# Four convolution layers on one core: weights laid out on the host, last stores on two queues, first columns loaded early, statistics by sums

## The chip, the core and the metric

The kernel runs on one of the eight cores of a Trainium2 chip. A core has five engines with instruction queues of their own: PE (matmuls), DVE (vector work), ACT (activations), POOL (vector work) and SP, which only issues transfers. ACT and POOL issue transfers too. All transfers run on the same 16 DMA engines. The metric is the device time of one execution in microseconds (us). Of the kernel before, three runs are shown: 3322.16, 3325.16 and 3326.02 us, median 3325.16.

## The reference

The input x is 8 images of 32 channels of 256 x 256 points, in float32. Four layers follow one another, each of the form x = x + f(norm(x)), where norm takes mean and variance over pairs of channels (16 groups).

```python
x = x + L0(gn(x))   # rfft2, 2 x 32 x 32 complex modes mixed over the channels, irfft2, + bias
x = x + L1(gn(x))   # one 5 x 5 kernel on every channel
x = x + L2(gn(x))   # a gated recurrence (GRU) over the columns w = 0 .. 255:
#   i = W_ih [prev(h-1), prev(h), prev(h+1)] + b_ih;   hh = W_hh cur + b_hh
#   r = sigmoid(r_i + r_h);  z = sigmoid(z_i + z_h);  n = tanh(n_i + r * n_h)
#   new = n * z + cur * (1 - z);  column 0 is kept as it is
x = x + L3(gn(x))   # running maxima from the 4 sides, joined with x, 1 x 1 convolution
```

## The kernel before

The work is a chain of stages with a normalisation between them, and so with a seam between them: the next stage's scale factors need all of the data of an image.

`forward_and_mix` (L78) is the transform of layer 0 and the mixing of its modes. It writes the spectrum to DRAM (smd, L290), half of the stores from ACT, half from SP.

`inverse_and_conv` (L296) is the inverse transform and layer 1. It goes through 16 units: image b and half h of the channels (L331), so units 14 and 15 belong to image 7. A unit has two halves of 8 channels (ch 0 and 1). Per unit there are eight groups g; a group's convolution is `conv_within` (L460) and `conv_across` (L468) on PE, DVE adds the result to x with sums (L483), ACT takes the squares (L489). After g = 3 and g = 7, `store` (L496) writes one half to x2d in DRAM as 36 transfers on SP's queue: 4 row classes a (partitions 32a to 32a+31) times 9 column blocks p, each of 28 to 30 partitions and 256-byte rows. `statistics` (L507) turns a unit's sums into mean and 1/deviation and copies them into stb[P, 3, B, A, C], four times for each of the four a (L530; L375 for the third kind). POOL computes the power -1/2 (L457, L527) and loads x for the units ahead (L382).

`recurrence` (L602) is layer 2. A partition is one (a, channel), where the row is 4q + a. Columns are taken in blocks of 8 (32 blocks), and each column in two chains x = 0, 1 of four images. Ahead of the loop, in this order on SP's queue: two bias loads (L645, L646), 16 loads of 12 KB that place the pieces of the recurrent weights in a zeroed tile (L626 to L642), then the x blocks (L677). 48 small matmuls turn stb so that each partition holds its own mean and factor (L655), DVE derives `sc` and `shift` (L663, L666). ACT normalises a block with 16 instructions (L686). In the loop, ACT normalises pieces of block bi+1 after every half step, and SP loads block bi+2 in the middle of block bi (L845). So the first normalisation of block 1 stands in ACT's order after the first block's 16 and ahead of the first gate (L786). After a block, `finish` stores it to x3d; `running` keeps the maxima from the left in the tiles fm (three buffers, L819) and stores them to fwd. Both are eight transfers of 256 KB from 32 partitions each, on SP (L811). `bn_stats` (L833) collects mean and spread of every 512 values, and `bn_aggr` (L857) joins the 32 records of each image at the end.

`maxima_and_mix` (L860) is layer 3. It loads its weights in eight transfers on SP (L876, L877), finishes the statistics in the helper `finish_stats` (L58), scales the weights (L889 to L915), and then goes through the blocks from the right, each loaded by SP from x3d and fwd (L933).

The order inside `manual_schedule` is the order in which the code issues. Outside of it (weights, constants, the small statistics between the stages) a planner orders the instructions by its own costs. An engine works off its own queue in order. A tile of a new stage takes the place of old ones, so its first writer waits until these have been read, transfers included.

Of the kernel before, what the change touches and what calls it, by code (L numbers as in the profile page):

```python
# [16 lines left out]
P = 128  # L17
# [6 lines left out]
A = 4  # L24
# [33 lines left out]
def finish_stats(tc, pool, psum, k, mv, n, lhsT, tag, ptag="stat", pbufs=1):  # L58


    nc = tc.nc
    sq = pool.tile([P, n], F32, name=f"sq_{tag}", tag=f"sq_{tag}")
    nc.vector.tensor_tensor(sq, mv[:, :, 0], mv[:, :, 0], ALU.mult)
    nc.vector.tensor_tensor(mv[:, :, 1], mv[:, :, 1], sq, ALU.add)
    ps = psum.tile([P, n, 2], F32, name=f"stat_{tag}", tag=ptag, bufs=pbufs)
    nc.tensor.matmul(ps, lhsT=lhsT, rhs=mv, start=True, stop=True)
    st = pool.tile([P, n, 2], F32, name=f"st_{tag}", tag=f"st_{tag}")
    nc.vector.tensor_copy(st, ps)
    sq2 = pool.tile([P, n], F32, name=f"sq2_{tag}", tag=f"sq2_{tag}")
    nc.vector.tensor_tensor(sq2, st[:, :, 0], st[:, :, 0], ALU.mult)  # L70
    ve = pool.tile([P, n], F32, name=f"ve_{tag}", tag=f"ve_{tag}")
    nc.vector.tensor_tensor(ve, st[:, :, 1], sq2, ALU.subtract)
    nc.vector.tensor_scalar(ve, ve, 0.0, EPS, ALU.max, ALU.add)
    nc.gpsimd.tensor_tensor(st[:, :, 1], ve, k.mhalf[:, :n], ALU.pow)
    return st, ve
# [219 lines left out]

def inverse_and_conv(tc, k, d, smd, xmean, x2d, stb):  # L296

# [15 lines left out]
    with ExitStack() as ctx:  # L313
# [43 lines left out]
        def spectrum(b):  # L357
# [15 lines left out]
            nc.vector.scalar_tensor_tensor(t[0:1, :, 0, 0], up[0:1], HW, t[0:1, :, 0, 0], ALU.mult, ALU.add)  # L373
            for a in range(A):
                nc.vector.tensor_copy(by_pair(stb[:, 2, b, a, :]), twice(m1, 4))  # L375

# [119 lines left out]
        def store(u, ch):  # L496
            b, h = units[u]
            c0 = 2 * CH * h + CH * ch
            for a in range(A):
                for p, t in enumerate(BLOCKS):  # L500
                    lo, hi = 0 if t == 0 else 2, 32 if t == NT - 1 else 30
                    nc.sync.dma_start(
                        out=x2d[b, a, c0 : c0 + CH, TS * t + lo : TS * t + hi].rearrange("c w q -> w c q"),
# [3 lines left out]
        def statistics(u):  # L507
# [20 lines left out]
            for kind in range(2):  # L528
                for a in range(A):
                    nc.vector.tensor_copy(  # L530
                        by_pair(stb[:, kind, b, a, 2 * CH * h : 2 * CH * (h + 1)]), twice(st[:, kind], 2)
                    )

# [14 lines left out]
        with tc.manual_schedule(engines=None):  # L548
# [19 lines left out]
            for u in range(n):  # L568
                for g in range(2 * G):
# [24 lines left out]
                    if g % G == G - 1:  # L594
                        store(u, g // G)
                if u + 1 < n:
                    scale(u + 1, 0)
                    squares(u + 1, 1, 1, 1, NT)
            statistics(n - 1)


def recurrence(tc, k, d, x2d, x3d, fwd, stb, mean1, mv3):  # L602

# [9 lines left out]
    with ExitStack() as ctx:  # L613
# [5 lines left out]
        def rows(i):  # L619
            return slice(32 * i, 32 * i + 32)  # L620

        weights = one.tile([P, 4, 3, 2 * C], F32, name="weights")
        nc.vector.memset(weights, 0.0)  # L626

        def put(kind, i, j, src):
            at = slice(32 * (j % 2), 32 * (j % 2) + 32)
            nc.sync.dma_start(out=weights[rows(i), kind, :, at], in_=src.rearrange("c (g o) -> c g o", g=3))  # L630

        def tap(t):
            return d["wihT"][32 * t : 32 * t + 32]

        for i in range(A):
            put(0, i, i, tap(1))
            put(0, i, i ^ 1, tap(2 if i % 2 else 0))
            put(1, i, i, d["whhT"])
        put(2, 1, 2, tap(0))
        put(2, 2, 1, tap(2))  # L640
        put(3, 3, 0, tap(0))
        put(3, 0, 3, tap(2))  # L642
        bih = one.tile([P, 3], F32, name="bih")
        bhh = one.tile([P, 3], F32, name="bhh")
        nc.sync.dma_start(out=bih, in_=d["bih"])  # L645
        nc.sync.dma_start(out=bhh, in_=d["bhh"])  # L646
        brz = one.tile([P, 3], F32, name="brz")
        nc.vector.tensor_tensor(brz[:, 0:2], bih[:, 0:2], bhh[:, 0:2], ALU.add)
        nc.vector.tensor_scalar_mul(brz[:, 2:3], brz[:, 1:2], -1.0)


        scp = ps.tile([P, 3, B], F32, name="scp", tag="r0")
        for kind in range(3):
            for b in range(B):
                nc.tensor.matmul(  # L655
                    scp[:, kind, b : b + 1],
                    lhsT=stb[:, kind, b].rearrange("p a c -> p (a c)"),
                    rhs=k.ident[:, 0:1],
                    start=True,
                    stop=True,  # L660
                )
        sc = one.tile([P, 3, B], F32, name="sc2")
        nc.vector.tensor_copy(sc, scp)  # L663
        nc.vector.tensor_copy(mean1, sc[:, 2])
# [10 lines left out]
        def load(bi):  # L675
            t = blk.tile([P, B, WB, Q], F32, name=f"xw_{bi}", tag="xw", bufs=4)
            nc.sync.dma_start(  # L677
                out=t.rearrange("p b w q -> p b (w q)"),
                in_=x2d[:, :, :, bi * WB : (bi + 1) * WB, :].rearrange("b a c w q -> (a c) b (w q)"),
            )  # L680
            raws[bi] = t
            norms[bi] = blk.tile([P, B, WB, Q], F32, name=f"xn_{bi}", tag="xn")
# [124 lines left out]
        def store(bi, dst, t):  # L807

            for a in range(A):
                for b2 in range(2):  # L810
                    nc.sync.dma_start(  # L811
                        out=dst[bi, :, a, b2].rearrange("(i c) n -> c i n", c=C),
# [3 lines left out]
        def running(bi, wi):  # L816
            def piece():
                if wi == 0:
                    tops[bi] = blk.tile([P, B, WB, Q], F32, name=f"fm_{bi}", tag="fm", bufs=3)  # L819
                t, x = tops[bi], raws[bi][:, :, wi]  # L820
# [15 lines left out]
        with tc.manual_schedule(engines=None):  # L836
# [17 lines left out]
            for piece in pieces[0] + pieces[1]:  # L854
                piece()
        for b in range(B):
            nc.vector.bn_aggr(mv3[:, b, :], bst[:, b])  # L857


def maxima_and_mix(tc, k, d, x3d, fwd, mv3, mean1, out):  # L860
# [5 lines left out]
    with ExitStack() as ctx:  # L866
# [6 lines left out]
        b3 = one.tile([P, 1], F32, name="b3")  # L873
        for j in range(4):
            q = slice(32 * j, 32 * j + 32)
            nc.sync.dma_start(out=w3[q], in_=d["w3T"].rearrange("(t c) o -> c t o", t=5))  # L876
            nc.sync.dma_start(out=b3[q], in_=d["b3"].unsqueeze(1))  # L877

# [129 lines left out]
def kernel(ctx: ExitStack, tc: tile.TileContext, d: dict, out: bass.AP):  # L1008
# [11 lines left out]
    with tc.tile_pool(name="later", bufs=1) as later:  # L1020
        stb = later.tile([P, 3, B, A, C], F32, name="stb")
        inverse_and_conv(tc, k, d, smd, xmean, x2d, stb)
        recurrence(tc, k, d, x2d, x3d, fwd, stb, mean1, mv3)
    maxima_and_mix(tc, k, d, x3d, fwd, mv3, mean1, out)
# [57 lines left out]


def arrays_of(inputs):
    a = {name: np.asarray(v) for name, v in inputs.items()}
# [15 lines left out]
        "conv": conv_tiles(a["L1_conv_kernel"]),  # L1101
        "wihT": a["L2_conv_weight_ih"][order3][:, order3].T,
        "bih": np.tile(a["L2_conv_bias_ih"][order3].reshape(3, C).T, (4, 1)),
        "whhT": a["L2_conv_weight_hh"][order3][:, order].T,
        "bhh": np.tile(a["L2_conv_bias_hh"][order3].reshape(3, C).T, (4, 1)),
        "w3T": w3[order][:, order5].T,
        "b3": a["L3_conv_b"][order],
    }
# [21 lines left out]
```

## Time and profile before

| | us |
|---|---|
| three runs, median (lowest, highest) | 3325.16 (3322.16, 3326.02) |
| the profiled execution | 3323.04 |
| its span, first to last instruction | 3321.0 |
| busy: PE, DVE, ACT, POOL | 2991.7, 2497.4, 1896.2, 843.6 |
| mean granted PE clock | 0.941 |
| convolution's last product ends | 1149.3 |
| first normalisation of the recurrence | 1188.19 |
| first gate of the recurrence | 1198.45 |
| recurrence's last bn_stats ends, bn_aggr ends | 2623.4, 2630.6 |
| first maximum of layer 3 (DVE) | 2648.49 |

Times in the trace count from the first instruction. The page has the busy share of each engine in 40 slices of 83 us; the timeline lists an engine's or a queue's instructions with their start and length and, in brackets, how long the engine had been idle and what released it; "SPq" is SP's queue, whose entries are the issuing of transfers, not their landing. The chain of work is followed back from the last instruction. The windows give busy time, granted PE clock, the busy share of the DMA engines and GB/s for a stretch.

### The profile page before, as it was taken

Reading aid. Unit: us, or ns where it says so; the run is one execution under the profiler, and the core shown is the slowest. Engines: PE = TensorE matmul, PEld = TensorE weight load, DVE = VectorE, ACT = ScalarE, POOL = GpSimd, SP = SyncE. Lnnn points to the kernel's source line nnn. Section 1 sums busy time; section 2 is a strip of 40 time slices with the busy share of each in tenths; the row PEclk is TensorE's granted clock in tenths of the full one; section 3 lists DMA queues with packets and bytes.
Section 4 is the critical chain, followed back from the end, with each engine's and each line's share of the span. In section 5 each row is a group of like instructions: output and inputs, shape, how many; then the busy total and the mean of one; then the engine's idle time right before and its main releaser. Section 6 shows DMA issues by size and latency. Waiting matters only on the chain.

```text
span 3321.0 us, 108063 instructions
## 1 busy us (share of the span) xinstructions
PE 2991.7 (90%) x45546; PEld 1618.8 (49%) x45546; DVE 2497.4 (75%) x5058; ACT 1896.2 (57%) x4362; POOL 843.6 (25%) x1211
## 2 busy tenths in 40 slices
PE   7975899999999969999999999999999577777776
PEld 4655344444444446666666666666666323333332
DVE  5742555565555448888888888888888799999998
ACT  3422556556556458888888888888888322222222
POOL 0110111111111024444444444444444200000000
PEclk9985999999999989999999999999999789888888
DMA  9978477777776435565555556655554678788885
GB/s 374 380 294 180 149 189 190 185 188 186 197 188 170 104 105 139 150 154 154 137 139 135 139 146 154 154 140 141 138 138 117 179 290 308 309 307 309 309 309 223
DMA packets 534102, 655.30 MB, mean 197 GB/s; under 512 B 395249, under 2 KB 396145, under 8 KB 507889
## 3 DMA queue, kind: packets, MB, share of 16 engines
q1 hardware_dynamic: 492528, 499.48, 53.5%
q0 software_dynamic: 15360, 79.70, 7.1%
q10 hardware_dynamic: 25728, 69.21, 5.3%
q8 instruction: 359, 5.88, 0.7%
q14 instruction: 127, 1.03, 0.1%
HBM read 371.44 MB, written 272.63 MB: 194 GB/s over the span
## 4 chain that ended last, share of the span: by engine, by line
PE 69%; DVE 20%; issue 6%; DMA 3%; SPq 1%; ACT 1%; POOL 1%; DVEq 0%; ACTq 0%; POOLq 0%
PE z L706 15%; PE r L706 12%; PE vp L464 7%; PE vp L472 7%; PE ni L706 6%; PE nh L706 6%; DVE rv L957 5%; PE up L420 4%; PE yp L134 3%; DVE dq L969 2%; DVE m L973 2%; DVE m L971 2%; DVE m L972 2%; DVE x L966 2%; PE tp L403 2%
## 5 line engine op out<-in xcount | busy, mean ns | idle before, releaser
L714 PE MATMUL r<-hs,weights 64*64 64x256 f32 x4080 | 550.6, 388 | 0.0
L801 POOL TENSOR_TENSOR xw<-xw,hs 128x256 f32<-128x256 f32 x512 | 350.8, 685 | 755.4 <-DVE hs L800 715.9
L714 PE MATMUL ni<-hs,weights 64*64 64x256 f32 x4080 | 526.0, 375 | 0.0
L714 PE MATMUL z<-hs,weights 64*64 64x256 f32 x4080 | 525.9, 376 | 0.0
L1003 ACT ACTIVATE ot<-o,bres 128x512 f32<-128x512 f32 x256 | 155.1, 689 | 544.7 <-PE o L987 538.1
L489 ACT ACTIVATE junk<-x 128x128 f32<-128x128 f32 (+1 forms) x384 | 202.8, 528 | 329.0 <-DVE x L483 322.9
L796 POOL TENSOR_TENSOR a<-zm,xn 128x256 f32<-128x256 f32 x510 | 371.5, 728 | 7.1 <-issue 6.1
L987 PE MATMUL o<-m,wsc 32*32 32x512 f32 x3072 | 239.0, 838 | 136.4 <-DVE m L973 105.9
L706 PE MATMUL z<-xn,weights 64*64 64x256 f32 x2040 | 331.4, 401 | 33.2 <-ACT xn L686 29.7
L428 DVE TENSOR_TENSOR x<-up,xb 128x512 f32<-128x512 f32 x288 | 185.1, 686 | 209.0 <-PE up L420 204.8
L787 DVE SCALAR_TENSOR_TENSOR n<-nh,bhh,rs 128x256 f32<-128x256 f32 x510 | 246.7, 484 | 104.8 <-ACT rs L786 86.9
L483 DVE SCALAR_TENSOR_TENSOR x<-vp,r,x 128x128 f32<-128x128 f32 (+2 forms) x512 | 236.7, 513 | 110.1 <-PE vp L472 109.9
L686 ACT ACTIVATE xn<-xw,shift,sc 128x256 f32<-128x256 f32 x512 | 298.3, 586 | 37.0 <-DMA xw<-x2d 37.0
L786 ACT ACTIVATE rs<-r,brz 128x256 f32<-128x256 f32 x510 | 241.8, 474 | 118.6 <-PE r L714 118.6
L706 PE MATMUL nh<-xn,weights 64*64 64x256 f32 x2040 | 306.4, 377 | 1.0 <-issue 1.0
L706 PE MATMUL r<-hs,weights 64*64 64x256 f32 x2040 | 306.6, 377 | 0.4 <-DMA xw<-x2d 0.2
L706 PE MATMUL r<-xn,weights 64*64 64x256 f32 x2040 | 305.5, 376 | 0.0
L706 PE MATMUL z<-hs,weights 64*64 64x256 f32 x2040 | 305.3, 376 | 0.0
L706 PE MATMUL ni<-hs,weights 64*64 64x256 f32 x2040 | 305.2, 375 | 0.0
L464 PE MATMUL vp<-x,c_conv 128*128 128x256 f32 (+2 forms) x768 | 288.6, 510 | 2.9 <-DVE x L483 2.9
L794 ACT ACTIVATE n<-n,bih 128x256 f32<-128x256 f32 x510 | 259.6, 509 | 44.3 <-DVE n L793 3.6
L714 PEld LDWEIGHTS ni<-hs,weights 64*64 64x64 f32 x4080 | 283.7, 133 | 0.3
(156 smaller groups left out, 6544.0 us busy)
## 6 DMA issues: line engine op xcount, KB each, us to landing
xb<-in_xl_dram POOLq DMA_DIRECT2D x96, 768.0 KB, 5.9
xa<-in_xt_dram SPq DMA_DIRECT2D x64, 1024.0 KB
xw<-x2d SPq DMA_DIRECT2D x32, 2048.0 KB
x3d<-xw SPq DMA_DIRECT2D x256, 256.0 KB
fwd<-fm SPq DMA_DIRECT2D x256, 256.0 KB
x<-x3d SPq DMA_DIRECT2D x32, 2048.0 KB
fw<-fwd SPq DMA_DIRECT2D x32, 2048.0 KB
out_dram<-ot ACTq DMA_DIRECT2D x64, 1024.0 KB
```

The source lines that it names most:

```text
L464: nc.tensor.matmul(vp, lhsT=k.conv[:, 0:P], rhs=pair_of(u, ch, g, lo, hi), start=True, stop=False)
L472: nc.tensor.matmul(vp[o], lhsT=k.conv[r, P : P + 64], rhs=pair_of(u, ch, g, lo, hi, q0, r), start=False, stop=True,)
L483: nc.vector.scalar_tensor_tensor(x, src, state[u]["r"][ch][:, g : g + 1], x, ALU.mult, ALU.add, accum_out=s1[:, 0, n, ch, g : g + 1])
L686: nc.scalar.activation(norms[bi][:, b, w], raws[bi][:, b, w], AF.Identity, bias=shift[:, b : b + 1], scale=sc[:, 1, b : b + 1])
L706: ins = nc.tensor.matmul(out[r], lhsT=weights[r, kind, gate, :], rhs=src[r], start=start, stop=stop)
L714: ins = nc.tensor.matmul(out[pairs[1 - i]], lhsT=weights[r, kind, gate, :], rhs=prev[r, :, q0 : q0 + Q], start=False, stop=stop,)
L786: rs = nc.scalar.activation(r, p["r"], AF.Sigmoid, bias=brz[:, 0:1])
L787: nhr = nc.vector.scalar_tensor_tensor(m, nh, bhh[:, 2:3], r, ALU.add, ALU.mult)
L794: nc.scalar.activation(m, m, AF.Tanh, bias=bih[:, 2:3])
L796: nc.gpsimd.tensor_tensor(a, zm, cur, ALU.mult)
L801: nc.gpsimd.tensor_tensor(raw, raw, new, ALU.add)
L987: nc.tensor.matmul(pts[b2][i][32 * j : 32 * j + 32].rearrange("p (w q) -> p w q", q=Q), lhsT=wsc[q, b2, t, :], rhs=src[j][q, b2], start=first,
```

## The change

Six edits, all around the stage borders:

- The host lays the recurrent weights out as the one tile that the kernel needs (`gru_tiles`). `recurrence_weights` loads it and the biases on ACT's queue, ahead of `inverse_and_conv`; memset and the 16 loads go.
- Of the very last half's 36 stores to x2d, those with odd p (16) are issued on ACT, the others (20) on SP.
- The first 8 columns have a tile of their own, `first`, outside the stages. Images 0 to 6 are loaded into it from POOL in unit 15 after g = 4; image 7 follows on SP in the place of the old first block's load.
- stb loses its dimension a (12 copies per image become 3), and 32 x 32 transposes on DVE take the place of the 48 matmuls.
- The maxima have two buffers instead of three. Of the last block's stores to x3d and fwd, those of the upper four images (b2 = 1) are issued on ACT.
- The eight `bn_aggr` become two products, two reductions and a scaling over the same records; `finish_stats` loses the two instructions that turned variance into mean square. Layer 3's weights come laid out by the host, in two loads on POOL instead of eight on SP.

```diff
 def finish_stats(...):
-    sq = pool.tile([P, n], F32, name=f"sq_{tag}", tag=f"sq_{tag}")
-    nc.vector.tensor_tensor(sq, mv[:, :, 0], mv[:, :, 0], ALU.mult)
-    nc.vector.tensor_tensor(mv[:, :, 1], mv[:, :, 1], sq, ALU.add)
...
+def flat(t):
+    return t.rearrange("p b w q -> p b (w q)")
+def first_columns(x2d, lo, hi):
+    return x2d[lo:hi, :, :, 0:8, :].rearrange("b a c w q -> (a c) b (w q)")
...
 # inverse_and_conv
-            for a in range(A):
-                nc.vector.tensor_copy(by_pair(stb[:, 2, b, a, :]), twice(m1, 4))
+            nc.vector.tensor_copy(by_pair(stb[:, 2, b, :]), twice(m1, 4))
...
-                    nc.sync.dma_start(
+                    (nc.scalar if 2 * u + ch == 2 * n - 1 and p % 2 else nc.sync).dma_start(
...
                     if g % G == G - 1:
                         store(u, g // G)
+                    if u == n - 1 and g == G:
+                        nc.gpsimd.dma_start(out=flat(first[:, 0 : B - 1]), in_=first_columns(x2d, 0, B - 1))
...
+def recurrence_weights(tc, pool, d):
+    nc = tc.nc
+    weights = pool.tile([P, 4, 3, 2 * C], F32, name="weights")
+    nc.scalar.dma_start(out=weights, in_=d["gru"])
+    bih = pool.tile([P, 3], F32, name="bih")
+    bhh = pool.tile([P, 3], F32, name="bhh")
+    nc.scalar.dma_start(out=bih, in_=d["bih"])
+    nc.scalar.dma_start(out=bhh, in_=d["bhh"])
+    brz = pool.tile([P, 3], F32, name="brz")
+    nc.vector.tensor_tensor(brz[:, 0:2], bih[:, 0:2], bhh[:, 0:2], ALU.add)
+    nc.vector.tensor_scalar_mul(brz[:, 2:3], brz[:, 1:2], -1.0)
+    return weights, bih, bhh, brz
...
 # recurrence (weights, put, tap, biases and the 48 matmuls taken out)
+        weights, bih, bhh, brz = loaded
+        turned = one.tile([P, 3, B, C], F32, name="turned")
+        nc.vector.transpose(turned.rearrange("p k b c -> p (k b c)"), stb.rearrange("p k b c -> p (k b c)"))
+        sc = turned[:, :, :, 0]
...
+            if bi:
+                t = blk.tile([P, B, WB, Q], F32, name=f"xw_{bi}", tag="xw", bufs=4)
+                nc.sync.dma_start(...)
+            else:
+                t = first
+                nc.sync.dma_start(out=flat(t[:, B - 1 : B]), in_=first_columns(x2d, B - 1, B))
...
-                    nc.sync.dma_start(
+                    (nc.scalar if bi == NB - 1 and b2 else nc.sync).dma_start(
                         out=dst[bi, :, a, b2].rearrange("(i c) n -> c i n", c=C),
...
-                    tops[bi] = blk.tile([P, B, WB, Q], F32, name=f"fm_{bi}", tag="fm", bufs=3)
+                    tops[bi] = blk.tile([P, B, WB, Q], F32, name=f"fm_{bi}", tag="fm", bufs=2)
...
-        for b in range(B):
-            nc.vector.bn_aggr(mv3[:, b, :], bst[:, b])
+        parts = bst.rearrange("p b n (h k) -> p b (n h) k", k=3)
+        n = 2 * NB
+        second = one.tile([P, B, n], F32, name="second")
+        nc.vector.tensor_tensor(second, parts[:, :, :, 1], parts[:, :, :, 1], ALU.mult)
+        nc.vector.scalar_tensor_tensor(second, parts[:, :, :, 2], n / float(W * Q), second, ALU.mult, ALU.add)
+        nc.vector.tensor_reduce(mv3[:, :, 0], parts[:, :, :, 1], AX.X, ALU.add)
+        nc.vector.tensor_reduce(mv3[:, :, 1], second, AX.X, ALU.add)
+        nc.vector.tensor_scalar_mul(mv3, mv3, 1.0 / n)
...
 # maxima_and_mix
-        for j in range(4):
-            q = slice(32 * j, 32 * j + 32)
-            nc.sync.dma_start(out=w3[q], in_=d["w3T"].rearrange("(t c) o -> c t o", t=5))
-            nc.sync.dma_start(out=b3[q], in_=d["b3"].unsqueeze(1))
+        nc.gpsimd.dma_start(out=w3.rearrange("p t o -> p (t o)"), in_=d["w3T"])
+        nc.gpsimd.dma_start(out=b3, in_=d["b3"])
...
 # the kernel's body
-        stb = later.tile([P, 3, B, A, C], F32, name="stb")
-        inverse_and_conv(tc, k, d, smd, xmean, x2d, stb)
+        stb = later.tile([P, 3, B, C], F32, name="stb")
+        first = later.tile([P, B, 8, Q], F32, name="first")
+        loaded = recurrence_weights(tc, later, d)
+        inverse_and_conv(tc, k, d, smd, xmean, x2d, stb, first)
```

On the host, `gru_tiles` writes the taps of W_ih and W_hh into a zeroed [128, 4, 3, 64] array, and w3 and b3 are repeated for the four row classes.

## The prediction

> **What bounds the kernel now.** On the page I read the busy slices first, then the chain that ended last. The chain is 69% PE, but the slices show where PE is not the limit: the dip at 249 to 332 us, the 6 at 1162 to 1245 us (convolution to recurrence, "seam 1") and the 5 at 2573 to 2656 us (recurrence to maxima, "seam 2").
>
> ```profile
> PE   7975899999999969999999999999999577777776
> ```
>
> Seam 1 in the timeline, SP's queue first, then DVE and ACT (columns: start, length, engine, line, work, count, [idle before <- releaser]):
>
> ```profile
> 1137.77 27.36 SPq L502 DMA_DIRECT2D x2d<-x  x59
> 1166.79 0.37 SPq L645 DMA_DIRECT2D bih<-in_bih_dram  x1
> 1167.21 0.42 SPq L646 DMA_DIRECT2D bhh<-in_bhh_dram  x1
> 1167.85 1.29 SPq L630 DMA_DIRECT2D weights<-in_wihT_dram  x2
> ...
> 1175.58 2.51 SPq L630 DMA_DIRECT2D weights<-in_wihT_dram  x4
> 1178.40 6.42 SPq L677 DMA_DIRECT2D xw<-x2d  x3
> ```
> ```profile
> 1167.12 0.70 DVE L626 MEMSET weights<- 128x768 f32 x1 [12.47 <-DMA x2d<-x]
> ...
> 1188.19 8.95 ACT L686 ACTIVATE xn<-xw,shift,sc 128x256 f32<-128x256 f32 x18 [37.04 <-DMA xw<-x2d]
> 1197.16 1.28 ACT L786 ACT_TABLE_LOAD   x1
> 1198.45 0.47 ACT L786 ACTIVATE rs<-r,brz 128x256 f32<-128x256 f32 x1
> ```
>
> The seam is one file of SP work. The last 34 stores, 0.46 us apart, run from 1149.49 to 1165.13; the last lands near 1166.5. Two bias loads follow, sixteen weight loads 0.64 us apart (to 1178.1), the first x block (1178.40, landed 1188.19: 9.8 us), 18 normalisations, the table load, and at 1198.45 the first gate. Seam 2:
>
> ```profile
> 2615.59 9.20 SPq L811 DMA_DIRECT2D x3d<-xw  x8
> 2624.89 8.92 SPq L811 DMA_DIRECT2D fwd<-fm  x8
> 2633.99 1.47 SPq L876 DMA_DIRECT2D w<-in_w3T_dram  x1
> ...
> 2639.75 0.35 SPq L933 DMA_DIRECT2D x<-x3d  x1
> ```
> ```profile
> 2623.42 7.16 DVE L857 BATCH_NORM_AGGREGATE mv<-bst 128x2 f32<-128x192 f32 x8
> ...
> 2648.49 0.43 DVE L955 COPY rv<-x 128x512 f32<-128x512 f32 x1 [5.09 <-DMA x<-x3d]
> ```
>
> Again SP sets the end: stores, eight small loads (5.4 us), then the load that DVE waits for, 8.7 us from issue. The statistics are done at 2643.4, 5.1 us early. Last the windows (clock, DMA share and GB/s at the end of each line), of the two kinds of store and of a store from all 128 partitions:
>
> ```profile
> 1155.00:1160.00 5.00, 5.00 (x25) 5.00 (x25) 0.00 (x0) 0.00 (x0) 0.00 (x0) 0.50 0.59 126
> 2625.00:2630.00 5.00, 0.00 (x0) 0.00 (x0) 5.00 (x7) 0.00 (x0) 0.00 (x0) 0.50 0.93 227
> 3314.00:3316.00 2.00, 0.00 (x0) 0.00 (x0) 0.00 (x0) 2.00 (x4) 0.00 (x0) 1.00 1.05 430
> ```
>
> The convolution's stores leave 0.41 of the DMA engines idle: SP's issuing limits them. The recurrence's stores keep the engines busy (0.93) at half the rate of the third line.
>
> **What the skill says.** (1) "Perfetto Trace Analysis", DMA Optimizations: where descriptor generation is the bottleneck, balance DMAs over the issuing engines. The share of 0.59 says that this holds at seam 1. (2) "SBUF — State Buffer", Door 1: 32 partitions reach 8 of the 16 ports, about 218 GB/s; 128 reach all, 436. The trace agrees: 227 against 430. (3) The same page, "Can I just issue two DMAs to hit both halves?": no, +6%. No line of before shows it; it decides seam 2. (4) "TensorE: Matmul & The Clock Gate", What's actually happening: an idle window of about 3.4 us halves the clock. The trace has 0.50 from 1155 to 1190 us, 1.00 after 1195.
>
> **Seam 1, step by step.** *Weights.* The 16 loads, two bias loads and the memset leave SP and DVE. Between landing (1166.5) and the x load (1178.4) that is 11.9 us; 0.3 stays as the wait's own cost. They become three ACT issues after ACT's last store of the spectrum (297.27), 0.37 us each; ACT is idle until 328.08. Their 0.39 MB take 1.0 us at 390 GB/s (the rate while x loads) beside SP's last spectrum store, whose landing at 301.8 starts the critical spectrum loads: 0 to +1.3, I take +0.4. DVE's bias sums wait for them with ten 0.13-us memsets behind, DVE being idle until 324.20: nothing; 1.6 if that cover went.
>
> *Stores.* Of 36, 20 stay on SP and 16 go to ACT behind its squares (end 1151.15). Issuing alone: SP 1149.49 + 19 x 0.46 = 1158.2, ACT 1151.15 + 16 x 0.46 = 1158.5 (ACT's own issues took 0.37 to 0.42, so 0.46 is the safe side). Full engines give 126/0.59 = 213 GB/s; the 1.76 MB left at 1151.2 end at 1159.5. With 1.8 us to landing: 1160.3 to 1161.3.
>
> *First columns.* The POOL load of 1.8 MB can start at 1130.8, when POOL's previous power ends; the data (units 0 to 13) landed long before. Behind it on POOL is only the last power at 1152.55, 21.8 us idle ahead of it: hidden. But it runs beside SP's stores of the first half. From 1055 to 1064 us a 1.57-MB load did that: 14 stores were issued in 9 us where 19.5 fit, 2.5 us lost. Scaled to 1.8 MB: 2.9 us. Today SP goes over from one half to the other at 1148.4 (1165.13 less 36 x 0.464) almost without a wait, so it would go over at 1151.3 and end 20 x 0.464 later, at 1160.6. Last landing 1162.4; the ends are 1160.3 (nothing lost) and 1165 (nearly no gain from the second queue).
>
> *Then who is late?* SP issues image 7's 256 KB at 1162.7 and block 1 at 1163.1. Block 1 lands after 9.8 us (as today's first block) plus 0.65 for the 256 KB: 1173.6. ACT starts from the scale factors: DVE 0.6 after the landing as today, the transpose of 768 columns 0.96 (L147 takes 0.72 for 512, L173 1.21 for 1024), 0.25 for two small ops, so 1164.2. It has its 16 normalisations done at 1172.2 (16 x 0.497); image 7 lands at about 1166, in time. The two normalisations of block 1 stand in ACT's order ahead of the first gate and wait to 1173.6. With 1.0 for both and 1.28 for the table the gate starts at 1175.9: **-22.6 us**. PE would idle some 3 to 4 us between its first products and the next step and may drop to the 0.50 of point 4: 0 to 1.5, I take +0.5.
>
> *At nothing:* the 48 transposing matmuls (8.8 us) end at 1160.7, inside the stores' time already. Fewer copies into stb save DVE some 0.6 us a unit, in a stage where PE is busy 83.0 of 83.0 us (996 to 1079). The maxima with two buffers: block 0's last such store is issued at 1254.8 and lands by 1257, block 2's first write comes at 1289 (1199.9 and two blocks of 44.5), 32 us later; uncovered it would stall each of 30 blocks.
>
> **Seam 2.** DVE: eight aggregations (7.16) become a product and a fused one over 512 (0.69 each), two reductions (0.69 by "VectorE: DVE Perf Modes", one element a cycle; 0.5 to 0.9) and a scaling (0.1): 2.9. Two ops in the helper go. The statistics end at 2634.6 to 2637.5, the later if the constants' memsets (2.8) come first: off the path. The two POOL loads wait for the old buffers (about 2626) and take 1.1 us ahead of POOL's power at 2628: hidden. Path: the last store lands at about 2637.2, the DMA share falling from 0.88 to 0.20 there. Both queues now start without SP's wait for the second chain (2616 to 2618.6, about 2 us at half-empty engines), and +6% on the remaining 3.7 MB gives 1: landing 2634.4, load 0.3 later, DVE 8.7 later: 2643.4, **-5.0**. Bounds: nothing gained by the queues -2.1; all ports open (landing 2628.5) -11.
>
> **Sum.** -22.6 + 0.5 + 0.4 - 5.0 = -26.7 us. On the profiled execution (3323.04: span 3321.0 and 2.0 around it) that is 3296.3; the median of the runs shown, 3325.16, is 2.1 higher: **3298**.
>
> **Rivals.** *Ports open* (0.20): two queues draw on different port halves. Landing 1160.3, gate 1173.8 (-24.6), seam 2 -11, cold and start +0.9: -34.7 against 3325.2, 3290. For it: SP is two stores ahead of ACT at seam 2, so the two read different partitions. Against: point 3. *Stores hardly faster* (0.20): both queues sit on the same 28 to 30 partitions; landing 1165, gate 1178.5 (-20), cold +1.5, start +1.3, seam 2 -2.1: -19.3, 3306. Against it: the idle 0.41. *The early load isn't early* (0.03): were x2d followed as a whole, it would wait for the first half's stores (1150.2) and the second half's for it (1158): landing 1169.3, gate 1182.7, 3305. Against it: today's stores into x2d don't wait for each other. *Slower* (0.02): the maxima's two buffers make DVE wait once a block. It outweighs the gain from 26.7/30 = 0.9 us a block on, which needs that store to land 33 us later; at 2 us a block 3298 + 60 = 3358. Against it: the 32 us of cover. The forecast's case has 0.53; 0.02 is left for no change.
>
> **Numbers.** About 0.2% (6.6 us) is what a measurement of this kernel tells from none. Faster 0.96, same 0.02, slower 0.02. The range takes in the three main cases: 3288 to 3308.
>
> **What would show it.** Right: no load between the last x2d store and x on SP; stores on SP and ACT together for some 9 us; the last wait before the first gate is ACT for block 1; its start 22 to 24 us earlier; at seam 2 DVE's copy still waits for the x load, some 5 us earlier. Wrong: first normalisation or gate waiting for the POOL load; SP's stores of the first half ending after 1153; a wait on the maxima in each block; seam 2 ending on POOL's weights.

## The result and the profile after

The changed kernel is slower: 3341.86 us (median of 6 runs, 3338.43 to 3343.99) against 3325.51 us for the kernel before in the same series (6 runs), a ratio of 1.0049 with a 95% interval of 1.0036 to 1.0062. The prediction was 3298 us, in a range of 3288 to 3308. The difference has the wrong sign.

The busy slices of the kernel after show where. The slice of 1169 to 1253 us, right behind the convolution, holds a 4 where before had a 6 (columns: busy tenths in 40 slices).

```profile
PE   7975899999999849999999999999999677777776
```

The timelines of SP's queue and of ACT at that place answer to those shown in the prediction (start, length, engine, line, work, count, [idle before <- releaser]; "ACTq" is the issuing on ACT's queue).

```profile
1160.48 49.03 SPq L507 DMA_DIRECT2D x2d<-x  x105
1209.55 0.40 SPq L669 DMA_DIRECT2D first<-x2d  x1
1210.95 1.00 SPq L664 DMA_DIRECT2D xw<-x2d  x2
```
```profile
1152.95 0.95 ACTq L507 DMA_DIRECT2D x2d<-x  x2
1153.94 6.56 ACTq L507 DMA_DIRECT2D x2d<-x  x14
1212.51 7.97 ACT L675 ACTIVATE xn<-first,shift,turned 128x256 f32<-128x256 f32 x16 [58.56 <-DVE shift L652]
1220.96 1.09 ACT L675 ACTIVATE xn<-xw,shift,turned 128x256 f32<-128x256 f32 x2 [0.47 <-DMA xw<-x2d]
1222.07 1.28 ACT L775 ACT_TABLE_LOAD   x1
1223.36 0.47 ACT L775 ACTIVATE rs<-r,brz 128x256 f32<-128x256 f32 x1
```

Read from the bottom, the second half of the seam is as predicted: no weight loads, the last block load, 16 normalisations, two for block 1, the table, the gate. What is wrong stands in the first line. When the convolution had ended, SP did not have 20 stores left but 105, and it began them only at 1160.48, in the moment in which ACT had issued its last one (1153.94 + 6.56 = 1160.50). SP's waits in the window from 1130 to 1212 us (total, times, longest) and the windows (clock, DMA share, GB/s at the end) say what it did before:

```profile
SPq L507 <- DMA x2d<-x: 52.0, 1, 52.0
```
```profile
1120.00:1125.00 5.00, 1.00 0.00 0
1125.00:1130.00 5.00, 1.00 0.00 0
1130.00:1135.00 5.00, 1.00 0.00 0
1135.00:1140.00 5.00, 1.00 0.52 129
...
1145.00:1150.00 5.00, 1.00 0.00 0
```

SP stood still for 52 us, from 1108 us on, in one wait for a store into x2d; this wait is called the stand below. In the windows shown no store moved at all; the 129 GB/s at 1135 us are the early load on POOL. Then the 105 stores went out 0.47 us apart (49.03 us in all), about the rate of before.

The table cuts four profiled executions into stretches. The two right columns belong to the first and the seventh experiment.

| stretch, us | before | after | E1 | E7 |
|---|---|---|---|---|
| to SP's last store of the mode mixing | 297.6 | 299.9 | 299.0 | 297.8 |
| to DVE's first work on the spectrum | 26.6 | 27.8 | 27.5 | 27.8 |
| to the convolution's end on DVE | 825.8 | 825.1 | 828.0 | 823.9 |
| to the last x2d store issued by SP | 15.1 | 56.7 | 20.3 | 14.4 |
| to the first gate | 33.3 | 13.8 | 14.2 | 14.0 |
| to the recurrence's last sum on POOL | 1419.6 | 1422.2 | 1423.6 | 1422.1 |
| to DVE's first maximum | 30.5 | 22.8 | 23.1 | 22.7 |
| to the end | 672.5 | 672.0 | 671.8 | 671.6 |
| span | 3321.0 | 3340.3 | 3307.7 | 3294.4 |

The stores lost 41.6 us. The rest of seam 1 gained 19.5 and seam 2 gained 7.7, while the recurrence's stretch took 2.6 more. In a single profile the first row differs by some 3 us among kernels that do the same there, and the recurrence's row by nearly 4 (E1 1423.6, E8 1419.8); smaller differences in these rows mean nothing.

### The profile page after: what moved, and what is told of

Read it like the earlier page. It is cut to its first block, busy times and chain, and to the rows that moved or that the text cites. A ratio compares the mean times of both kernels' runs of the same rounds, so it can differ in the third digit from the quotient of the medians.

```text
span 3340.3 us, 107823 instructions
## 1 busy us (share of the span) xinstructions
PE 2986.9 (89%) x45498; PEld 1609.8 (48%) x45498; DVE 2486.5 (74%) x4932; ACT 1896.3 (57%) x4362; POOL 845.6 (25%) x1214
## 4 chain that ended last, share of the span: by engine, by line
PE 72%; DVE 19%; issue 3%; DMA 3%; SPq 2%; ACT 1%; POOL 0%; ACTq 0%; DVEq 0%; POOLq 0%
PE z L695 15%; PE r L695 12%; PE vp L469 8%; PE vp L477 8%; PE nh L695 6%; PE ni L695 6%; DVE rv L951 5%; PE up L425 4%; PE yp L131 3%; DVE dq L963 2%; DVE m L967 2%; DVE m L965 2%; DVE x L960 2%; DVE m L966 2%; PE tp L408 2%
## 5 line engine op out<-in xcount | busy, mean ns | idle before, releaser
L790 POOL TENSOR_TENSOR xw<-xw,hs 128x256 f32<-128x256 f32 x496 | 339.8, 685 | 698.1 <-DVE hs L789 696.7
L675 ACT ACTIVATE xn<-xw,shift,turned 128x256 f32<-128x256 f32 x496 | 290.3, 586 | 0.5 <-DMA xw<-x2d 0.5
```

The source lines that it names most:

```text
L675: nc.scalar.activation(norms[bi][:, b, w], raws[bi][:, b, w], AF.Identity, bias=shift[:, b : b + 1], scale=sc[:, 1, b : b + 1])
L790: nc.gpsimd.tensor_tensor(raw, raw, new, ALU.add)
```

## The experiments

Each ran against the kernel before in the same series. Ratios are to it, with 95% intervals.

The theory comes from the compiled program, that is from its list of instructions with their waits; no trace shows the counters themselves, so the runs test what follows from them. In that list, each transfer that SP or ACT issues is counted on one of eight counters. They are dealt out in turn over both queues, in the order in which the planner expects the transfers, and a transfer waits until the one eight places ahead of it has landed. POOL's transfers are counted elsewhere. In that order the two queues do not fit together: the planner puts ACT's 16 stores of the last half, which cannot start before the convolution's end, among SP's stores of unit 14's first half. From 105 stores before its end, SP waits for ACT's.

**E1: all of the convolution's stores on SP**

```diff
-                    (nc.scalar if 2 * u + ch == 2 * n - 1 and p % 2 else nc.sync).dma_start(
+                    nc.sync.dma_start(
```

> The kernel after with all of the convolution's stores on SP again; every other part of the change stays. Theory (SP's stores waited for the 16 that ACT issues): SP's 52-us stand at 1108 us is gone, the last store lands at about 1169 to 1172 (before: 1166.5; the conv ends 2.5 us later and the early POOL load takes 0 to 3 us), the gate starts 13.5 us later, at 1182 to 1186, against 1223.4 after and 1198.5 before; time 3300 to 3305 us, 20 to 25 below before. Rival (the early load on POOL holds x2d's writers up): the stand stays, time 3338 to 3346. Rival (the two queues' transfers were slow, not held): last landing near 1169 too, but no stand to lose, so this kernel could not tell it; its mark would be stores more than 0.46 us apart here.

Measured: 3305.65 us, ratio 0.9935 (0.9923 to 0.9948). The stand is gone. SP's and ACT's timelines:

```profile
1097.94 76.95 SPq L507 DMA_DIRECT2D x2d<-x  x144
1174.94 0.40 SPq L669 DMA_DIRECT2D first<-x2d  x1
```
```profile
1189.12 0.47 ACT L775 ACTIVATE rs<-r,brz 128x256 f32<-128x256 f32 x1
```

SP's stores run through to 1174.9; the gate is at 1189.1, 3 us later than expected, since this execution's convolution ended late (1154.6, in the kernel after 1152.8) and the stores took 20.3 us from there. Undoing one line turns the change from 16 us slower to 21.6 us faster than before (3327.25 in this series).

**E2: the kernel before with that line alone**

```diff
-                    nc.sync.dma_start(
+                    (nc.scalar if 2 * u + ch == 2 * n - 1 and p % 2 else nc.sync).dma_start(
```

> The kernel before with one edit: 16 of the last half's 36 stores on ACT. Theory: SP stands from about 1106 us until ACT's stores have landed at 1158 to 1160, then issues some 105 stores 0.46 us apart, to 1207; the gate follows the last landing by 32 us as before, at 1240 to 1243; time 3367 to 3371 us, 42 to 46 above before. Rival (the early load is the cause): no stand, last landing 1161 as the prediction had it, time 3319 to 3322.

Measured: 3365.93 us, ratio 1.0115 (1.0101 to 1.0129), 38.7 us more than before and somewhat less than expected. SP's waits between 1085 and 1225 us, and line 502's instructions from 1150 us on (kind, count, shortest/median/longest ns, first and last start):

```profile
SPq L502 <- DMA x2d<-x: 53.0, 1, 53.0
```
```profile
L502 SPq DMA_DIRECT2D x2d<-x x105: 307/415/453, 1158.3 to 1206.7; - x105
```

The same stand and the same 105 stores, without an early load or any other part of the change. The line alone is enough.

**E3: the 16 stores on POOL in place of ACT**

```diff
-                    (nc.scalar if 2 * u + ch == 2 * n - 1 and p % 2 else nc.sync).dma_start(
+                    (nc.gpsimd if 2 * u + ch == 2 * n - 1 and p % 2 else nc.sync).dma_start(
```

> The kernel after with the 16 stores on POOL's queue in place of ACT's. Theory (SP waits for ACT's transfers because these two queues share the order in which transfers are counted off; POOL's do not): no stand; POOL takes about 1.0 us a store (its early load took 1.00), so they end at 1168 to 1170, gate 1182 to 1188, time 3300 to 3308 us. Rival (any second queue that writes x2d holds SP's writes to x2d): SP stands as long or longer, time 3340 us or more.

Measured: 3299.75 us, ratio 0.9917 (0.9903 to 0.9930). No stand; the gate is at 1180.7. POOL's timeline:

```profile
1134.61 1.00 POOL L601 DMA_DIRECT2D first<-x2d  x1 [2.08 <-DMA x2d<-x]
1150.57 0.69 POOL L507 DMA_DIRECT2D x2d<-x  x1 [14.95 <-DVE x L488]
1151.55 9.13 POOL L507 DMA_DIRECT2D x2d<-x  x15 [0.29 <-DVE x L488]
```

A second queue that writes x2d does not hold SP as such. POOL took 0.61 us a store, less than I had expected from its early load (1.00). Yet SP's own last 20 stores ended only at 1167.1, 15.3 us after the convolution, as late as 36 of them had ended in the kernel before. The later runs ask why.

**E4: no early load, the stores still on ACT**

```diff
-                    if u == n - 1 and g == G:
-                        nc.gpsimd.dma_start(out=flat(first[:, 0 : B - 1]), in_=first_columns(x2d, 0, B - 1))
...
-                nc.sync.dma_start(out=flat(t[:, B - 1 : B]), in_=first_columns(x2d, B - 1, B))
+                nc.sync.dma_start(out=flat(t), in_=first_columns(x2d, 0, B))
```

> The kernel after without the early load on POOL: SP loads the first columns of all eight images after the last store; the 16 stores stay on ACT. Theory: the stand stays, last store issued at 1208 to 1210; then block 0's load (9.8 us) and 18 normalisations in line (9 us) put the gate 8 to 10 us after that of the kernel after, time 3349 to 3353 us. Rival (the early load is the cause): the stand is gone, last landing 1163, gate about 1184, time 3300 to 3306 us.

Measured: 3350.05 us, ratio 1.0066 (1.0053 to 1.0080). SP stands 53.1 us, and from the last store to the gate it takes 20.9 us against 13.8 in the kernel after. The early load is not the cause; it is worth 7.1 us of that stretch in these two traces.

**E5: a single store on ACT**

```diff
-                    (nc.scalar if 2 * u + ch == 2 * n - 1 and p % 2 else nc.sync).dma_start(
+                    (nc.scalar if 2 * u + ch == 2 * n - 1 and p == 1 and a == 0 else nc.sync).dma_start(
```

> The kernel after with a single one of the last half's 36 stores on ACT (the one of the first row block's second piece); the other 35 are on SP. Theory (what counts is that SP's later stores wait for ACT's, not how many): SP stands from about 1098 us until that one store has landed, 1154 to 1156, then has some 129 stores to issue 0.46 us apart, to 1214 to 1216; gate 1227 to 1230, time 3343 to 3351 us, no better than with sixteen. Rival (the loss grows with the number of stores on ACT or with their own slowness): nearly all of the loss is gone, time 3304 to 3310 us.

Measured: 3345.05 us, ratio 1.0059 (1.0046 to 1.0072). ACT's one store, SP's wait between 1085 and 1225 us, and line 507 from 1150 us on:

```profile
1152.65 0.59 ACTq L507 DMA_DIRECT2D x2d<-x  x1
```
```profile
SPq L507 <- DMA x2d<-x: 50.9, 1, 50.9
```
```profile
L507 SPq DMA_DIRECT2D x2d<-x x129: 307/417/600, 1154.4 to 1214.1; - x129
```

One store of 56 KB does as much harm as sixteen. The count is the theory's, and it was expected before the run: in the compiled program's list this store has place 1151, SP's next store on the same counter has 1159, the last 1287, and that makes 129. With sixteen it is 105, as the kernel after and E2 have it. SP goes on 1.2 us after ACT's issuing ends.

**E6: all stores on SP, the early load one unit sooner**

```diff
-                    if u == n - 1 and g == G:
+                    if u == n - 2 and g == 0:
```

> All of the convolution's stores on SP, as in the first run, and the early load moved forward on POOL: out of the last unit into the first group of the unit before, where SP waited 9.8 us for DVE (1085 to 1095 us). Theory (at 1137 us the early load delayed SP's stores by some 5 us, last issue 20.4 us after the end of the convolution against 15.2 before): it runs at 1087 to 1097 us, the last issue is 15 to 16 us after the convolution's end, time 3299 to 3303 us, 4 to 6 less than the first run. Rival (the last stores are limited by SP's issuing alone and the early load cost nothing): time 3304 to 3308 us, as the first run.

Measured: 3299.94 us, ratio 0.9921 (0.9907 to 0.9934). SP's last store is issued 16.0 us after the convolution's end against 20.3 in E1. So at its place in the change the early load cost SP's stores 4.3 us; moved to where SP waits for DVE, it leaves 16.0 us against 15.1 in the kernel before. The windows of E1 at 1140 us show the collision (DMA share, GB/s at the end):

```profile
1140.00:1145.00 5.00, 1.00 0.97 282
1145.00:1150.00 5.00, 1.00 0.76 198
1150.00:1155.00 5.00, 1.00 0.59 125
```

**E7: 16 stores on POOL and the early load sooner**

Both edits together, of E3 and of E6.

> Sixteen of the last half's stores on POOL, as in the third run, and the early load moved forward as in the run before this one. Theory: SP reaches its own 20 stores of the last half when the convolution ends instead of 6 us later, last issue 10 us after the end of the convolution (third run: 15.4), gate 13.6 us later; time 3292 to 3296 us. Rival (POOL's and SP's stores together are limited by the DMA engines, 0.76 to 0.87 busy in the third run): last issue no earlier than 13 us after the convolution's end, time 3297 to 3300 us.

Measured: 3297.89 us, ratio 0.9919 (0.9906 to 0.9933). The rival was right: the last issue comes 14.4 us after the convolution's end, not 10. Windows of E7:

```profile
1150.00:1155.00 5.00, 0.87 0.81 134
1155.00:1160.00 5.00, 0.50 0.84 151
1160.00:1165.00 5.00, 0.50 0.66 135
```

Two queues raise the DMA engines' busy share from 0.59 to 0.84, but the rate only from 126 GB/s to between 134 and 151. SP's 20 stores are now 0.7 us apart in place of 0.46, although from 1140 to 1166 us SP waits 0.3 us in all for anything ahead of them. Why they go out more slowly is not shown, nor why E3, with the same two queues, reached 180 GB/s at a share of 0.87 (1155 to 1160 us). A second queue on POOL brings 1.6 us here (14.4 against 16.0), and in time nothing that can be measured against E6.

**E8: E1 with the recurrence's last stores on SP too**

```diff
-                    (nc.scalar if bi == NB - 1 and b2 else nc.sync).dma_start(
+                    nc.sync.dma_start(
```

> The first run's kernel with the recurrence's last stores (x3d and fwd) back on SP, so that both of the change's second queues are undone. Theory (as the prediction split it): the weights' loads taken off SP give some 5.4 of the 7.3 us by which this seam is shorter in the first run, the second queue the other 2; time 3306 to 3310 us against 3305.65, DVE's first copy 25 us after the recurrence's last sum against 23.1. Rival (two queues draw on different port halves): the second queue gives 5 or more, time 3310 to 3314 us.

Measured: 3308.93 us, ratio 0.9949 (0.9936 to 0.9961). From the recurrence's last sum to DVE's first maximum 26.6 us against 23.1 in E1: 3.4 us in the traces, more than the 2 of the theory and less than the 5 of the rival. Of the 7.3 us by which this seam is shorter in E1 than before, 3.9 are left for the weights' loads and the rest. The times alone don't part E1 and E8.

**E9: the kernel before with the host's weights alone**

```diff
-        weights = one.tile([P, 4, 3, 2 * C], F32, name="weights")
-        nc.vector.memset(weights, 0.0)
...
+        loaded = recurrence_weights(tc, later, d)
```

> The kernel before with one part alone: the recurrence's weights laid out by the host and loaded on ACT at the end of the mode mixing. The prediction's step: SP's last store to the first gate 11.6 us shorter than the 33.3 of before, the spectrum 0.4 us (0 to 1.3) later. From the kernel after and the runs so far (DVE's first spectrum work 27.4 to 27.8 us after SP's last mode-mixing store, before 26.6) I now expect the start to cost 0.8 to 1.2. Time 3314 to 3317 us. Rival (the weight loads lay beside the landing of the stores and cost little): seam 30 us or more, time 3322 us or more.

Measured: 3316.54 us, ratio 0.9973 (0.9962 to 0.9985). SP's last store to the gate takes 22.2 us in place of 33.3 (predicted 11.6 less, measured 11.1); the start takes 28.1 us in place of 26.6. This run also shows something that nobody expected. Seam 2 takes 27.3 us in place of 30.5 without any edit there: SP issues seven of layer 3's eight small loads between its first two stores to x3d, while it waits for the recurrence's last sum. And that last sum comes late, behind a memset of the next stage (E11 has the lines): from POOL's last product to the end of its last sum 4.47 us pass, against 2.50 in the kernel before and in E2. So the weights' part alone, far away from it, changed the planner's order at the end of the recurrence.

**E10: E7 with the weights loaded later, on POOL**

```diff
+                    if u == 1 and g == 0:
+                        for t, name in zip(loaded, ("gru", "bih", "bhh")):
+                            nc.gpsimd.dma_start(out=t, in_=d[name])
```

The two bias sums move to the start of the recurrence's code.

> The seventh run's kernel with the recurrence's weights and biases loaded later: on POOL, in the second unit of the convolution, and the two bias sums at the start of the recurrence. Theory (the weights' 0.39 MB and the two bias loads ahead of the spectrum's loads cost the start about 1 us): DVE's first spectrum work 26.3 to 26.8 us after SP's last mode-mixing store against 27.4 to 27.8; time 3296 to 3298 us against 3297.9. Rival (that 1 us comes from the throttle or from the order of the spectrum's loads): 27.4 or more, no difference in time.

Measured: 3305.95 us, ratio 0.9941 (0.9929 to 0.9954), 8 us more than the theory allows. The start did become shorter (26.8 us), but the convolution took 831.2 us against 823.9. DVE's waits from 405 to 432 us hold:

```profile
DVE brz L643 <- DMA bhh<-in_bhh_dram: 2.7, 1, 2.7
```

The planner had put the bias sum, which nothing needs for 700 us, straight behind the loads, in the middle of DVE's work for the convolution. DVE waited 2.7 us with the inverse transform's sums behind it, and PE was idle 1.7 us of the stretch from 415 to 420 us.

**E11: E10 with the fills of cuts and top made late**

```diff
-        nc.vector.memset(cuts, BIG)
+        first = mv3.rearrange("p b k -> p (b k)")[:, 0:1]
+        nc.vector.tensor_scalar(
+            cuts.rearrange("p s w q -> p (s w q)"), first.to_broadcast([P, 4 * WB * QP]), 0.0, BIG, ALU.mult, ALU.add
+        )
```

The same goes for top. The reason lies in the kernel after, in DVE's timeline at the end of the recurrence:

```profile
2641.83 0.42 DVE L788 TENSOR_TENSOR n<-n,nh 128x256 f32<-128x256 f32 x1
2642.21 0.07 DVE L895 MEMSET sel<- 128x8 f32 x1
2642.66 1.82 DVE L914 MEMSET cuts<- 128x2112 f32 x1 [0.39 <-DVE n L788]
2644.39 0.36 DVE L789 TENSOR_TENSOR hs<-n,a 128x256 f32<-128x256 f32 x1
```

A memset of the next stage stands ahead of DVE's sum that POOL's last one waits for; in the kernel before, it stood behind the statistics (2631.20 us, `bn_aggr` ending at 2630.6).

> The run before this one, with the fills of cuts and top made after the statistics (from a value of theirs, times 0, plus or minus the constant) in place of the memsets. Theory (in the kernel after, DVE does the 1.82-us memset of cuts ahead of the recurrence's last sum and holds that back by 2.0 us): POOL's last sum ends 2 us sooner after DVE's last product; time 2 us less than the run before this one, 3294 to 3296 us. Rival (the last sum waits for POOL's product, not for DVE): no difference.

Measured: 3301.43 us, ratio 0.9924 (0.9911 to 0.9938). From the start of POOL's last product to the end of its last sum 2.98 us against 4.47 in E10 and 2.50 before: 1.5 us, not 2.0. The 4.5 us between the medians of E10 and E11 is more than this explains; the intervals overlap.

**E12: E11 with the recurrence's last stores on SP**

The edit of E8.

> The run before this one with the recurrence's last stores all on SP. Theory (the first run against the eighth: 23.1 against 26.6 us from the recurrence's last sum to DVE's first copy): the second queue is worth 3 to 4 us there; time 3297 to 3300 us. Rival (the eighth run's difference was chance, one queue fills the DMA engines as two do): difference under 1 us. Rival (two queues draw on different port halves): 6 us or more.

Measured: 3308.25 us, ratio 0.9942 (0.9930 to 0.9955). 26.9 us from the last sum to the first maximum against 23.9 in E11, so the second queue is worth 3.0 us by the traces, as the theory had it. The time lies 6.8 us above E11's and outside the range expected; the traces don't explain more than the 3.0. DMA rates just behind the recurrence's end, first E11, then E12:

```profile
2610.00:2615.00 5.00, 0.50 0.98 259
2615.00:2620.00 5.00, 0.50 0.94 284
```
```profile
2610.00:2615.00 5.00, 0.50 0.97 225
2615.00:2620.00 5.00, 0.50 0.93 235
```

**E13: stores on ACT at their right place in the order**

```diff
-                    nc.sync.dma_start(
+                    (nc.scalar if u >= n - 2 and p % 2 else nc.sync).dma_start(
```

This is E6 with 64 stores on ACT.

> The sixth run's kernel (early load moved forward) with 16 of every 36 stores on ACT in the last two units, 64 stores in place of the kernel after's 16. In the compiled program ACT's stores of each half now stand among SP's stores of the same half, where in the kernel after the 16 stand among SP's of three halves earlier. Theory (what held SP was the place of ACT's stores in the shared order): no stand on ACT's stores, SP waits some 10 us for DVE at 1085 us as in the sixth run and little else, last issue 12 to 17 us after the convolution's end, time 3294 to 3302 us. Rival (any stores on ACT beside SP's hold SP up, because ACT issues them behind its own work): SP's wait on stores is 30 us or more again, time 3325 us or more.

Measured: 3314.25 us, ratio 0.9957 (0.9944 to 0.9971). The mark that tells the theories apart is clear; the time lies between the two. SP's waits from 1070 to 1190 us, then ACT's from 1080 to 1190 us:

```profile
SPq L507 <- DVE x L488: 35.5, 10, 17.4
SPq L507 <- DMA x2d<-x: 15.8, 18, 3.7
```
```profile
ACT junk L494 <- DMA x2d<-x: 23.4, 2, 11.8
```

SP's longest wait on a store is 3.7 us, not 52: stores on ACT don't hold SP if their place fits. Now the shared order works the other way. ACT stands up to 11.8 us in its stores with the squares of the next groups behind them, and the convolution ends at 1170.2 in place of 1150.3. The last half's 36 stores, issued by both, then take 12.8 us from the convolution's end, against 16.0 for SP alone, although SP still waits 4.7 us for landings in that time. While both issue, the rate is higher than with POOL in E7:

```profile
1175.00:1180.00 5.00, 0.50 0.89 188
```

**E14: E7 with the late fills of E11**

> The seventh run's kernel with the late fills of the eleventh. Theory (the 1.82-us memset ahead of the recurrence's last sum costs 2 us): 2 to 4 us less than the seventh run, 3294 to 3296 us; if the eleventh run's gain over the tenth was chance, 3297 to 3299 us.

Measured: 3298.27 us, ratio 0.9915 (0.9901 to 0.9929). POOL's last product to its last sum's end takes 2.98 us as in E11, against 4.48 in E7. A gain of 1.5 us is too small for the times to show: no difference from E7.

**E15: E14 with the weights on POOL and the bias sums two units later**

```diff
+                    if u == 3 and g == 0:
+                        _, bih, bhh, brz = loaded
+                        nc.vector.tensor_tensor(brz[:, 0:2], bih[:, 0:2], bhh[:, 0:2], ALU.add)
+                        nc.vector.tensor_scalar_mul(brz[:, 2:3], brz[:, 1:2], -1.0)
```

> The run before this one with the weights loaded on POOL in the second unit as in the tenth run, and the two bias sums written into the convolution's own order two units later. In the tenth run DVE waited 2.7 us for the bias load in the middle of the convolution, ahead of the inverse transform's sums, and the convolution took 831 us against 824. Theory (that wait was the tenth run's whole loss): the convolution takes 824 to 826 us, the start is 1 us shorter, time 3293 to 3295 us. Rival (POOL's queue or the loads' traffic cost it): the convolution takes 829 us or more, 3299 us or more.

Measured: 3299.24 us, ratio 0.9921 (0.9909 to 0.9934). The start takes 26.5 us against 28.0, the convolution 827.2 against 824.0 in E14 and 831.2 in E10. It lies between the two theories. DVE's wait was part of E10's loss; what the rest is stays open, since the convolution's stretch differs by 2.5 us also between E1 and E8, which do the same there.

## Why the prediction was wrong

**The step that failed** is the first sentence of *Stores*: "Of 36, 20 stay on SP and 16 go to ACT behind its squares", with "Issuing alone: SP 1149.49 + 19 x 0.46 = 1158.2". It took SP's queue up to the convolution's end as it was before, and ACT's queue as one beside it; a wait of one for the other was put at nothing. That is false. SP's stores wait for ACT's, and by the planner's order they do so from 105 stores before SP's end. E1 and E2 show that this one line makes the loss (36 us when it is taken out, 39 when it is put in), E3 and E4 clear the second queue as such and the early load, E5 shows that the count on ACT doesn't matter, and E13 that the place does. The predicted last landing of 1162.4 us became a last issue at 1209.5: SP's 105 stores took 49.0 us behind ACT's 16.

A line of the trace before could have raised the question. Over the whole run, SP's stores into x2d waited not only for DVE but also so:

```profile
SPq L502 <- DMA x2d<-x: 46.9, 38, 2.6
```

They already waited, 38 times and up to 2.6 us, for the landing of other stores into x2d. Against the rival *The early load isn't early* the prediction said that "today's stores into x2d don't wait for each other". They do; the waits were only short while one queue issued them all in order. Who waits for whom once a second queue comes in was the question to ask; the line alone does not answer it.

**What the second queue is worth without the hold stays open.** "Full engines give 126/0.59 = 213 GB/s" took the idle 0.41 of the DMA engines as room. The point that I named for it, from the Trainium skill's "Perfetto Trace Analysis", DMA Optimizations (balance transfers over the issuing engines), brought 1.6 us with POOL as the second queue: E7 filled 0.25 of the idle share with 8 to 25 GB/s, and there the rival *Stores hardly faster* was right. With ACT as the second queue E13 had 188 GB/s at a share of 0.89, which scales to 211 as the prediction had it, and took 3.2 us less than SP alone, at the price of ACT's stands. ACT beside SP with neither of them held was not run.

**First columns.** The load cost SP 4.3 us, not 2.9 (E1 against E6), in the same way as the prediction worked it out. It was issued at 1135.62, 2.1 us after POOL's previous power had ended, for 1130.8 predicted; it brought 7.1 us of seam 1 (E4). E6 shows a place where SP's stores end 16.0 us after the convolution, 0.9 later than without any early load.

**Then who is late?** Right. Block 1 ended the wait (0.47 us of ACT's idle time in the kernel after). Last issue to gate is 13.8 us, 1.5 us less than in the prediction (1175.9 less 1160.6). With the convolution's stores left on SP, the other terms come out within the range: E1 is 3305.65, near its upper end, E6 with the early load moved is 3299.94.

**Weights.** E9: 11.1 us for 11.6. The start cost 0.8 to 1.5 us wherever the weights load on ACT (27.4 to 28.1 us for 26.6), for 0.4 predicted and a bound of 1.3 (the three issues on ACT, priced at 0.37 us each, took 0.38, 2.40 and 0.64 in the kernel after); where they are moved away it is 26.3 to 26.8, as before. That the weights' part would move a memset to the end of the recurrence (E9) was not in the prediction.

**Seam 2.** First gate to first maximum is 1444.9 us against 1450.0 before, -5.1 for -5.0, but that agreement is luck. Seam 2 itself is 7.7 us shorter and the recurrence's stretch 2.6 longer. Of the 7.7, E9 has 3.2 without any of this seam's edits, and 3.0 to 3.4 are the second queue, for 2.9 predicted. These shares come from different kernels and need not add up. Of the 2.6, only the late last sum is seen: 4.46 us against 2.50 from POOL's last product to its last sum's end in the kernel after, of which E11 and E14 won back 1.5. The statistics by sums are off the path, as predicted; the two reductions, priced at 0.69 us each, took 0.82 and 0.69. The Trainium skill's "SBUF — State Buffer", "Can I just issue two DMAs to hit both halves?", gives +6% for two transfers on both halves; here, with many stores waiting on each queue, it was 259 and 284 against 225 and 235 GB/s (E11 and E12), 15 and 21% more. The measurement decides. The rival *Ports open* asked for more and fell. Waits on the two fm buffers come to no more than 0.4 us in all.

**The rivals** missed the cause as well. *Slower* had a chance of 0.02 and another mechanism. All cases took it for granted that a transfer moved to another queue leaves the first queue alone.

Of the versions tried, E3, E6, E7, E14 and E15 are 0.8% faster than before and not to be told apart. E3 and E6 are the simplest: the change with the 16 stores on POOL in place of ACT, or with all of the convolution's stores left on SP and the early load one unit sooner.

## What to carry to other kernels

Moving a transfer to a second queue can put a wait on the first: where the program counts landings in an order that both queues share, a late transfer placed early in that order stops the other queue's transfers behind it. Before costing such a move, look in the trace for the first queue's waits on its own earlier transfers, and afterwards count what it has left when it goes on. And read an instruction outside the hand-written order, a memset, a bias sum, as one that the planner may put in the worst place; what stands behind it on its engine is its price.

## What the runs showed of the hardware

- How much of the DMA engines' idle share a second queue turned into rate differed from run to run. For stores of 28 to 30 partitions and 256-byte rows, SP alone gave 126 GB/s at a share of 0.59; SP and POOL gave 134 to 151 at 0.81 to 0.84 in E7, but 180 at 0.87 in E3; SP and ACT gave 188 at 0.89 in E13.
- For stores of 256 KB from 32 partitions, two queues gave 259 and 284 GB/s (E11) where one gave 225 and 235 (E12), at about the same busy share of the DMA engines (0.94 to 0.98 and 0.93 to 0.97).
- POOL issued one of the convolution's stores every 0.61 us (E3), SP every 0.46 (the kernel before), ACT every 0.47 (14 in 6.56 us, the kernel after).
- Issuing the two small bias loads took ACT 2.40 and 0.64 us in the kernel after, behind the weights' load (0.38), where SP took 0.37 and 0.42 for them in the kernel before.
